# Layer 0's first four token blocks in a written-out order, and the products beside the latents dealt out anew

## The chip, the cores and the metric

The kernel runs on one core of a Trainium2 chip. The metric is the device time of one execution in microseconds (us); lower is better. The core's engines work beside each other: TensorE (PE, with its weight loads shown as PEld), VectorE (DVE), ScalarE (ACT), GpSimd (POOL) and SyncE (SP), which issues most of the DMAs. Each works through its own instructions in the order in which they were written and waits on semaphores for the others.

## The reference, cut to what matters

Two layers over 4 sequences of 256 tokens with 512 features (1024 tokens, eight blocks of 128). What the change touches is at the start of layer 0 and, with one list of numbers, at the second half of its tokens:

```
x = L0_attn_x                         # (4, 256, 512)
xn = _layernorm(x, axis=-1)
x = x + _L0_attn_ref(xn, ...) + _L0_ffn_ref(xn, W_gate, W_up, W_down)
xn = _layernorm(x, axis=-1)
x = x + _L1_attn_ref(xn, ...) + _L1_ffn_ref(xn, ...)

# _L0_attn_ref
C_q = x @ Wq_d + bq_d                 # 12 latent features
C_kv = x @ Wkv_d + bkv_d              # 4 latent features
q = (C_q @ W_qk + b_qk).reshape(b, s, 32, 4)
scores = einsum('bqhd,bkd->bhqk', q, C_kv) / sqrt(4)
out = einsum('bhqk,bkhd->bqhd', softmax(scores), V)
# _L0_ffn_ref
h = silu(x @ W_gate.T) * (x @ W_up.T) # 1792 hidden features
out = h @ W_down.T
```

Layer 1 is a selective scan (a state-space block) and a mixture of low-rank experts. The change does not touch it.

## The kernel before

**Tiling.** Layer 0 handles the tokens in two halves (`th` 0 and 1) of four blocks of 128. A half is two sequences (`b` 0, 1 and 2, 3). The order of every instruction is written out by hand: Python calls and generators give it, and `go(gen, n)` takes `n` steps of a generator.

**First four blocks** (lines 534 to 549). Each block of `x` is normalized: `ln_stats` (DVE: statistics L207, L208), `ln_root` (ACT: square root, L212), `ln_scale` (DVE: reciprocal L218, `xn` L221). `ln_turn` has PE turn the block in four transposes (L243) into a PSUM tile `pt`, and ACT copies it out twice: `xhi` (L245, rounded for the fast product type) and `xnT` (L246, whole). `ln_rest` (L252, DVE) writes `xlo`, the difference of `pt` and `xhi`. Products of the feed-forward read `xhi` and `xlo`; the latents read `xnT`. The PSUM pool `psmm` has three buffers of tag "mm", which `pt`, the latents' products and the feed-forward's share; `pssc` has two of tag "sc" for score products.

**The latents** (`latents(b)`, L289) are a generator of nine steps for one sequence: `pl` (L294, four products that need two blocks of `xnT`) with its copies on ACT (`kT` L297, `ks` L298, `cq` L300); the split of the key on DVE (`ks`, L302); `pkm` (L307) and its copy `km` (L308); `pq` (L313) with `q`, `qhi` on ACT (L317, L320); `qlo` on DVE (L322) and `pz` (L327); and four times `pqg` (L336) with its copy `qg` (L338). Before, the first step of the first latents stands inside the loop over blocks, behind the turn of block 2 and ahead of the turn of block 3.

**The feed-forward** `ff` is a generator too. In the first half it is `gate_up(0)` (L431): one step is one pair of products `pg` or `pu` (L445, `xhi` and `xlo` with one chunk of weights); four steps fill one PSUM tile, then ACT and DVE make `g` (L452, L453, L455), ACT `hhi` (L456) and POOL `hlo` (L457). The weights `wgu` come by POOL's DMAs into four buffers, three tiles ahead. In the second half, while the latents run, it is `down(0, i)`: one step is a pair `po` (L470), and the first step of a block is the product with `m_att` (L465).

**Maxima** (`maxima`, L559): for eight `k`, two score products `sc` (L353, eight matmuls in all) and their maxima on DVE (L355), a number of steps of `ff` from the list `pieces`, at three `k` a `put_max` (L365, L372), and one step of the second sequence's latents. Then `attention` follows. The totals of `ff` steps up to the attention are 41 in the first half (9 beside the latents, 32 in the maxima) and 35 in the second (9 and 26).

Of the kernel before, what the change touches and what calls it, by code (L numbers as in the profile page):

```python
# [8 lines left out]
F32 = mybir.dt.float32  # L9
# [8 lines left out]
P = 128  # L18
# [3 lines left out]
HC = D // P  # L22
# [19 lines left out]
def block_kernel(  # L42
# [24 lines left out]
    nc = tc.nc  # L67
    mm = nc.tensor.matmul
# [16 lines left out]
    ident = cst[:, C_ID : C_ID + P]  # L85
# [8 lines left out]
    psmm = ctx.enter_context(tc.tile_pool(name="psmm", bufs=3, space=PSUM))  # L94
    ps0 = ExitStack()
    pssc = ps0.enter_context(tc.tile_pool(name="pssc", bufs=2, space=PSUM))
# [79 lines left out]
    def fold_load():  # L176
        live["wvt"] = ffn.tile([P, 4, P], F32, tag="g", name="wvt", bufs=2)
        nc.sync.dma_start(live["wvt"], wvt_d)
        live["wo"] = ap1.tile([P, 4, D], F32, tag="pe", name="wo", bufs=2)
        nc.sync.dma_start(live["wo"], wo_d)  # L180
        nc.sync.dma_start(bo, bo_d)
# [12 lines left out]
    tok = {}  # L194
# [9 lines left out]
    def ln_stats(th, i):  # L204
        mv = tok[th][2]
        st = ap1.tile([P, 6], F32, tag="ln_st", name="st", bufs=2)
        nc.vector.bn_stats(st, x[:, 4 * th + i, :])  # L207
        nc.vector.bn_aggr(mv[:, i, :], st)  # L208

    def ln_root(th, i, n):  # L210
        mv, rs = tok[th][2:]
        nc.scalar.activation(rs[:, i : i + n], mv[:, i : i + n, 1], AF.Sqrt, bias=eps[:, 0:1])  # L212

    def ln_scale(th, i, n):
        mv, rs = tok[th][2:]
        if th == 0 or i == 0:
            m = n if th == 0 else 4
            nc.vector.reciprocal(rs[:, i : i + m], rs[:, i : i + m])  # L218
        for k in range(i, i + n):
            xn = ap1.tile([P, D], F32, tag="ln_xn", name="xn", bufs=2)  # L220
            nc.vector.tensor_scalar(  # L221
                xn, x[:, 4 * th + k, :], mv[:, k, 0:1], rs[:, k : k + 1], ALU.subtract, ALU.mult
            )
            tok[th, k] = xn
# [14 lines left out]
    def ln_turn(th, i):  # L239
        xnT, (hi, lo) = tok[th][:2]  # L240
        pt = psmm.tile([P, HC, P], F32, tag="mm", name="pt")
        for hc in range(HC):
            nc.tensor.transpose(pt[:, hc, :], tok[th, i][:, hc * P : (hc + 1) * P], ident)  # L243
        w = slice(i * P, (i + 1) * P)
        nc.scalar.copy(hi[:, :, w], pt)  # L245
        nc.scalar.copy(xnT[:, :, w], pt)  # L246
        tok[th, i] = pt

    def ln_rest(th, i):
        hi, lo = tok[th][1]  # L250
        w = slice(i * P, (i + 1) * P)
        nc.vector.tensor_tensor(lo[:, :, w], tok[th, i], hi[:, :, w].bitcast(F32), ALU.subtract)  # L252
# [93 lines left out]
    def scores_max(b, k, hp):  # L346

        gq, qb = k // 2, k % 2
        sc = pssc.tile([P, 2, 512], F32, tag="sc", name="sc")
        for hf in range(2):  # L350
            for i in range(2):
                w = rows(2 * hp + i)
                mm(sc[:, i, hf * S : (hf + 1) * S], lhsT=qs[b][w, gq, hf, qb * P : (qb + 1) * P],  # L353
                   rhs=kms[b][w], start=True, stop=True)
        nc.vector.tensor_reduce(  # L355
            mpl2[b % 2][:, qb, 2 * hp : 2 * hp + 2, 16 + 2 * gq : 18 + 2 * gq],
            sc.rearrange("p i (f k) -> p i f k", f=2), AX.X, ALU.max,
        )

    def put_max(b, gq):  # L360


        pm = psmm.tile([P, S], F32, tag="mm", name="pmT")
        for qb in range(2):
            nc.tensor.transpose(  # L365
                pm[:, qb * P : (qb + 1) * P], mpl2[b % 2][:, qb].rearrange("p h r -> p (h r)"),
                ident,
            )
        for hf in range(2):
            g = 2 * gq + hf  # L370
            q = qs[b][:, gq, hf, :]
            nc.vector.scalar_tensor_tensor(  # L372
                q, pm, mask[:, g : g + 1], q.bitcast(F32), ALU.mult, ALU.add
            )
# [56 lines left out]
    def gate_up(th):  # L431


        hi, lo = hids[th]
        xs = tok[th][1]
        for m in range(MC):
            for k in range(2):
                i = th * NW + 2 * m + k
                load_w(i + 3)
                if th == 0 and k == 0 and m % 2 == 1:  # L440
                    nc.gpsimd.dma_start(wd[:, m - 1 : m + 1, :], wd_d[:, m - 1 : m + 1, :])
                ps = psmm.tile([P, 512], F32, tag="mm", name="pg" if k == 0 else "pu")
                for hc in range(HC):
                    for j in range(2):
                        mm(ps, lhsT=wgus[i][:, hc, :], rhs=xs[j][:, hc, :],  # L445
                           start=(hc == 0 and j == 0), stop=(hc == HC - 1 and j == 1))
                    if hc < HC - 1:
                        yield

                if k == 0:  # L450
                    g = ffn.tile([P, 512], F32, tag="g", name="g", bufs=2)
                    nc.scalar.activation(g, ps, AF.Tanh, scale=0.5)  # L452
                    nc.vector.scalar_tensor_tensor(g, g, 1.0, ps, ALU.add, ALU.mult)  # L453
                else:
                    nc.vector.scalar_tensor_tensor(g, g, 0.5, ps, ALU.mult, ALU.mult)  # L455
                    nc.scalar.copy(hi[:, m, :], g)  # L456
                    nc.gpsimd.tensor_tensor(lo[:, m, :], g, hi[:, m, :].bitcast(F32), ALU.subtract)  # L457
                yield
# [26 lines left out]
    def go(gen, n=1000):  # L485
        for _ in range(n):
            if next(gen, 1) == 1:
                break
# [7 lines left out]
    def attention(b, ff, after, step, side=()):  # L496


        side = dict(side)
        for k in range(8):  # L500
            attend(b, k, 0)
            if after:
                scores_max(b + 1, k, 1 - k // 2 % 2)
            elif k:
                attend(b, k, 1)
            if after or k == 0:
                go(ff, step - step // 2)
            if k == 0:
                put_max(b, 3)
                go(ff, 3)  # L510
            elif after and k in (3, 5, 7):
                put_max(b + 1, k // 2 - 1)
            if after or k == 0:
                attend(b, k, 1)
            if after:
                scores_max(b + 1, k, k // 2 % 2)
            if k:
                weigh(b, k - 1)
            elif b % 2:
                weigh(b - 1, 7)  # L520
            go(ff, step // 2 if after or k == 0 else step)
            for f, *args in side.get(k, ()):
                f(*args)
# [12 lines left out]
        ln_stats(0, i)  # L536
        ln_root(0, i, 1)
    first, second = latents(0), latents(1)
    for i in range(4):
        ln_scale(0, i, 1)  # L540
        ln_turn(0, i)
        if i == 2:
            go(first, 1)
        if i < 2:
            ln_stats(0, i + 2)
            ln_root(0, i + 2, 1)
        if i:
            ln_rest(0, i - 1)
    ln_rest(0, 3)
    nc.scalar.preload_act_table_set("exp_and_others")  # L550
    fold_load()
    for tb in range(4, NTB):
# [3 lines left out]
    ff = gate_up(0)  # L556
    masks()

    def maxima(b, pieces, second, side=()):  # L559

        side = dict(side)
        for k in range(8):
            for hp in range(2):
                scores_max(b, k, hp)
            for f, *args in side.get(k, ()):
                f(*args)
            go(ff, pieces[k])
            if k in (3, 5, 7):
                put_max(b, k // 2 - 1)
            go(second, 1)  # L570
        go(second)

    for _ in range(9):
        go(first, 1)
        go(ff, 1)
    maxima(0, (5, 5, 1, 6, 1, 5, 5, 4), second, {2: [(fold_att, 0)], 4: [(fold_att, 1)]})
    attention(0, ff, True, 5)
    norm = normalize(0)
    attention(1, ff, False, 3, {
# [9 lines left out]
    ff = (0 for i in range(4) for _ in down(0, i))  # L589
# [5 lines left out]
    for i in range(4):  # L595
        ln_turn(1, i)
        if i == 1:
            ln_scale_act(1, 2, 2)
        go(ff, 3)
        ln_rest(1, i)  # L600
    first, second = latents(2), latents(3)
    for i in range(9):
        go(first, 1)
        go(ff, 1)
        if i == 5:
            pre_stats(0)
    maxima(2, (4, 3, 3, 5, 3, 3, 3, 2), second, {
        2: [(pre_stats, 1)], 3: [(pre_scale,)], 5: [(pre_turn, 0)], 7: [(pre_turn, 1)],
    })
    go(ff)  # L610
# [1 line left out]
    ff = gate_up(1)  # L612
# [742 lines left out]
    ff = (0 for i in range(4) for _ in down(1, i))  # L1355
# [407 lines left out]
    for u in range(total + 2):  # L1763
# [6 lines left out]
        elif u > total:  # L1770
            b, c = B - 1, DC - 1
# [111 lines left out]
```

## Time and profile before

| | us |
|---|---|
| median of 3 runs | 820.84 |
| lowest, highest | 815.27, 824.40 |
| the profiled execution, its own time | 817.16 |
| its span | 814.9 |

The profile is of one execution. Its span counts from the first to the last instruction; its own time is 2.3 us longer. Times in the text are counted from the span's start. The stages by the windows of the trace: the first blocks and latents to 32.0 us, maxima of sequence 0 to 65.1, attention and feed-forward of the first half to 151.5, latents of the second half to 165.9, their maxima to 194.6, the rest of layer 0 and the entry of layer 1 to about 345, and layer 1's scan to the end.

How to read it: a line of the timeline gives start, duration, engine, line of the code, operation, tiles and shapes, and in brackets the idle time before it with what ended it. `L294` is line 294. A record of PE stands for one pass, so the four products of `pl` show as eight. The granted clock is the rate that TensorE's throttle let through, 1.00 being full speed.

### The profile page before, as it was taken

Reading aid. Unit: us, or ns where it says so; the run is one execution under the profiler, and the core shown is the slowest. Engines: PE = TensorE matmul, PEld = TensorE weight load, DVE = VectorE, ACT = ScalarE, POOL = GpSimd, SP = SyncE. Lnnn points to the kernel's source line nnn. Section 1 sums busy time; section 2 is a strip of 40 time slices with the busy share of each in tenths; the row PEclk is TensorE's granted clock in tenths of the full one; section 3 lists DMA queues with packets and bytes.
Section 4 is the critical chain, followed back from the end, with each engine's and each line's share of the span. In section 5 each row is a group of like instructions: output and inputs, shape, how many; then the busy total and the mean of one; then the engine's idle time right before and its main releaser. Section 6 shows DMA issues by size and latency. Waiting matters only on the chain.

```text
span 814.9 us, 11167 instructions
## 1 busy us (share of the span) xinstructions
PE 722.6 (89%) x3778; PEld 424.3 (52%) x3778; DVE 653.3 (80%) x589; ACT 552.2 (68%) x1122; POOL 515.8 (63%) x419
## 2 busy tenths in 40 slices
PE   4999999999999999989788888799888779889876
PEld 2665545566555586656446456454356345334331
DVE  4486756368654525998999999999999999999996
ACT  4335565434556347789998898989978897955642
POOL 4133232001333351758998999989799999889875
PEclk9799999999999999999979799899999889999989
DMA  7233432000322433366677627544547553464610
GB/s 232 65 93 90 130 91 77 1 1 14 78 78 78 120 65 104 103 164 191 186 186 196 177 68 200 142 106 104 180 102 158 119 141 104 117 143 118 127 40 27
DMA packets 72802, 92.02 MB, mean 113 GB/s; under 512 B 12733, under 2 KB 54793, under 8 KB 72618
## 3 DMA queue, kind: packets, MB, share of 16 engines
q1 hardware_dynamic: 61226, 67.98, 31.4%
q0 software_dynamic: 10800, 21.50, 11.1%
q10 hardware_dynamic: 720, 1.84, 0.6%
q8 instruction: 30, 0.49, 0.3%
q14 instruction: 26, 0.21, 0.1%
HBM read 68.67 MB, written 13.43 MB: 101 GB/s over the span
## 4 chain that ended last, share of the span: by engine, by line
PE 40%; DVE 36%; ACT 10%; issue 4%; POOL 4%; DMA 3%; SPq 1%; POOLq 0%; ACTq 0%; DVEq 0%
DVE h L1123 15%; DVE bx L1106 12%; PE pg L445 7%; PE pu L445 5%; DVE x L1123 4%; PE av L398 4%; PE px L793 4%; ACT decay L1091 3%; PE po L470 3%; POOL h L1128 2%; PE scT L387 2%; DVE mpl L355 2%; PE po L1328 2%; PE ysum L1146 1%; DMA dus<-dud 1%
## 5 line engine op out<-in xcount | busy, mean ns | idle before, releaser
L1128 POOL TENSOR_TENSOR h<-h,cr 128x1024 f32<-128x1024 f32 (+1 forms) x105 | 245.6, 2345 | 34.2 <-DVE h L1123 24.1
L1123 DVE TENSOR_TENSOR_SCAN h<-decay,bx 128x1024 f32<-128x1024 f32 (+1 forms) x101 | 224.1, 2222 | 3.6
L1091 ACT ACTIVATE decay<-dts,aneg 128x255 f32<-128x255 f32 x492 | 205.4, 499 | 30.6 <-DVE h L1123 19.1
L1106 DVE TENSOR_TENSOR bx<-brow,dus 128x1024 f32<-128x1024 f32 x128 | 157.6, 1231 | 9.7 <-ACT decay L1091 4.6
L457 POOL TENSOR_TENSOR hlo<-g,hhi 128x512 fp32r<-128x512 f32 x28 | 35.9, 1282 | 114.5 <-ACT hhi L456 114.5
L1146 PE MATMUL ysum<-h,stack 128*32 128x256 f32 x824 | 69.3, 412 | 33.1 <-POOL h L1128 32.7
L355 DVE TENSOR_REDUCE mpl<-sc 128x4 f32<-128x1024 f32 x64 | 76.7, 1218 | 22.6 <-PE sc L353 21.2
L428 POOL DMA_DIRECT2D wgu<-in_wgu x56 | 31.0, 556 | 95.2 <-PE pg L445 94.3
L389 ACT ACTIVATE pe<-scT 128x1024 f32<-128x1024 f32 x64 | 64.0, 1023 | 22.9 <-PE sc L353 14.2
L793 PE MATMUL px<-xn1T,w_in 128*128 128x256 f32 x256 | 63.8, 401 | 8.1 <-ACT xn1T L781 4.0
L1328 PE MATMUL po<-ow,xc 128*128 128x512 f32 x128 | 66.7, 645 | 0.9 <-DVE xc L1776 0.4
L1056 PE MATMUL pz<-xn1T,w_in 128*128 128x256 f32 x256 | 64.6, 399 | 0.6 <-ACT sz L1067 0.6
L1128 POOL TENSOR_TENSOR x<-x,cr 128x1024 f32<-128x1024 f32 x24 | 57.8, 2406 | 6.4 <-DVE x L1123 3.9
L793 PEld LDWEIGHTS px<-xn1T,w_in 128*128 128x128 f32 x256 | 50.2, 200 | 20.8 <-ACT xn1T L781 4.5
L1146 PEld LDWEIGHTS ysum<-h,stack 128*32 128x32 f32 x824 | 18.2, 111 | 78.3 <-POOL h L1128 52.1
L1056 PEld LDWEIGHTS pz<-xn1T,w_in 128*128 128x128 f32 x256 | 49.2, 199 | 18.0 <-issue 8.7
L1123 DVE TENSOR_TENSOR_SCAN x<-decay,bx 128x1024 f32<-128x1024 f32 x24 | 54.9, 2286 | 0.8
L453 DVE SCALAR_TENSOR_TENSOR g<-g,pg 128x512 f32<-128x512 f32 x28 | 19.2, 687 | 43.0 <-ACT g L452 43.0
L445 PE MATMUL pg<-xhi,wgu 128*128 128x512 f32 x112 | 49.6, 443 | 1.2 <-ACT xhi L245 1.2
L470 PE MATMUL po<-wd,hhi 128*128 128x512 f32 x112 | 49.6, 443 | 0.0
L456 ACT CAST hhi<-g 128x512 fp32r<-128x512 f32 x28 | 17.3, 619 | 45.8 <-DVE g L455 45.8
L445 PE MATMUL pu<-xhi,wgu 128*128 128x512 f32 x112 | 47.5, 424 | 0.8 <-DVE g L455 0.8
(244 smaller groups left out, 1399.6 us busy)
## 6 DMA issues: line engine op xcount, KB each, us to landing
dts<-dtd SPq DMA_DIRECT2D x124, 128.0 KB, 3.0
dus<-dud SPq DMA_DIRECT2D x124, 128.0 KB, 3.3
wgu<-in_wgu POOLq DMA_DIRECT2D x56, 256.0 KB, 2.8
w_in<-in_inz SPq DMA_DIRECT2D x16, 512.0 KB, 5.2
w_in<-in_inx SPq DMA_DIRECT2D x14, 512.0 KB, 4.4
dtd<-dt SPq DMA_DIRECT2D x15, 256.0 KB, 2.6
dud<-du SPq DMA_DIRECT2D x15, 256.0 KB, 2.2
wd<-in_wd POOLq DMA_DIRECT2D x7, 512.0 KB, 3.5
```

The costliest lines, as they stand in the source:

```text
L355: nc.vector.tensor_reduce(mpl2[b % 2][:, qb, 2 * hp : 2 * hp + 2, 16 + 2 * gq : 18 + 2 * gq], sc.rearrange("p i (f k) -> p i f k", f=2), A ...
L389: nc.scalar.activation(pes[b, k][:, 2 * t : 2 * t + 2, :], sc, AF.Exp)
L445: mm(ps, lhsT=wgus[i][:, hc, :], rhs=xs[j][:, hc, :], start=(hc == 0 and j == 0), stop=(hc == HC - 1 and j == 1))
L470: mm(po, lhsT=hids[th][j][:, m, i * P : (i + 1) * P], rhs=wd[:, m, :], start=False, stop=(m == MC - 1 and j == 1))
L793: mm(px[:, i, :], lhsT=w[:, i, hc, :], rhs=xns[b][:, hc, :], start=(hc == 0), stop=(hc == HC - 1))
L1056: mm(pz[:, i, :], lhsT=w[:, i, hc, :], rhs=xns[b][:, hc, :], start=(hc == 0), stop=(hc == HC - 1))
L1091: made["da", u] = nc.scalar.activation(da[:, k, 1:], live["dts", b, c][:, k, 1:], AF.Exp, scale=aneg[:, c, k, g : g + 1])
L1106: nc.vector.tensor_tensor(bx, brow[g // 2][:, g % 2, :].unsqueeze(1).to_broadcast([P, NG, S]), live["dus", b, c], ALU.mult)
L1123: nc.vector.tensor_tensor_scan(h[:, n].rearrange("p n t -> p (n t)"), da[:, n].rearrange("p n t -> p (n t)"), bx[:, n].rearrange("p n t -> ...
L1128: made["hc", u] = (nc.vector if k == NG - 1 else nc.gpsimd).tensor_tensor(h[:, n], h[:, n], crows[b][:, g, :].unsqueeze(1).to_broadcast([P ...
L1146: made["sum", u] = mm(ysum[k * NB : (k + 1) * NB, :], lhsT=stack, rhs=hc[:, k, :], start=False, stop=(g == NU - 1))
L1328: mm(live["po", b, i], lhsT=xcs[b][:, c, i * P : (i + 1) * P], rhs=late_w["ow"][:, c, :], start=first, stop=last)
```

## The change

Three new functions split `ln_turn` for the first half: `first_turn` (PE's transposes alone; block 3 takes its PSUM tile from the "sc" buffers), `first_high` (the copy `xhi`) and `first_whole` (the copy `xnT`). The loop over the four blocks is replaced by a written-out order in which all four turns come before the first step of the latents. The steps of `ff` beside the latents are no longer one each: 3, 0, 1, 2, 2, 1, 1, 1, 1 (and 0 for an extra last step in the first half, since the latents' first step has moved there). Beside the latents there are now 12 steps of `ff` in either half, and three fewer in the maxima, one less at `k` 0, 3 and 6.

```
+    def first_turn(i):
+        if i < 3:
+            pt = psmm.tile([P, HC, P], F32, tag="mm", name="pt")
+        else:
+            pt = pssc.tile([P, 2, 512], F32, tag="sc", name="pt")[:, 0, :].rearrange(
+                "p (c k) -> p c k", c=HC
+            )
+        for hc in range(HC):
+            nc.tensor.transpose(pt[:, hc, :], tok[0, i][:, hc * P : (hc + 1) * P], ident)
+        tok[0, i] = pt
+
+    def first_high(i):
+        nc.scalar.copy(tok[0][1][0][:, :, i * P : (i + 1) * P], tok[0, i])
+
+    def first_whole(i):
+        nc.scalar.copy(tok[0][0][:, :, i * P : (i + 1) * P], tok[0, i])
...
-    for i in range(4):
-        ln_scale(0, i, 1)
-        ln_turn(0, i)
-        if i == 2:
-            go(first, 1)
-        if i < 2:
-            ln_stats(0, i + 2)
-            ln_root(0, i + 2, 1)
-        if i:
-            ln_rest(0, i - 1)
+    ln_scale(0, 0, 1)
+    first_turn(0)
+    ln_stats(0, 2)
+    ln_root(0, 2, 1)
+    ln_scale(0, 1, 1)
+    first_high(0)
+    first_turn(1)
+    ln_stats(0, 3)
+    ln_root(0, 3, 1)
+    first_high(1)
+    ln_scale(0, 2, 1)
+    first_turn(2)
+    first_whole(0)
+    ln_scale(0, 3, 1)
+    first_turn(3)
+    ln_rest(0, 0)
+    first_high(2)
+    ln_rest(0, 1)
+    first_whole(1)
+    first_high(3)
+    ln_rest(0, 2)
     ln_rest(0, 3)
+    first_whole(2)
+    first_whole(3)
...
-    for _ in range(9):
+    for n in (3, 0, 1, 2, 2, 1, 1, 1, 1, 0):
         go(first, 1)
-        go(ff, 1)
-    maxima(0, (5, 5, 1, 6, 1, 5, 5, 4), second, {2: [(fold_att, 0)], 4: [(fold_att, 1)]})
+        go(ff, n)
+    maxima(0, (4, 5, 1, 5, 1, 5, 4, 4), second, {2: [(fold_att, 0)], 4: [(fold_att, 1)]})
...
-    for i in range(9):
+    for i, n in enumerate((3, 0, 1, 2, 2, 1, 1, 1, 1)):
         go(first, 1)
-        go(ff, 1)
+        go(ff, n)
         if i == 5:
             pre_stats(0)
-    maxima(2, (4, 3, 3, 5, 3, 3, 3, 2), second, {
+    maxima(2, (3, 3, 3, 4, 3, 3, 2, 2), second, {
```

## The prediction

> **What bounds the kernel now.** I read the page's busy shares first, then its windows cut by stage and, around the changed places, by the steps of the granted clock, then the order of time of these places. Busy times stand behind each stretch as length, PE, PEld, DVE, ACT, POOL, then granted clock, DMA share, GB/s.
>
> ```profile
> PE 722.6 (89%) x3778; PEld 424.3 (52%) x3778; DVE 653.3 (80%) x589; ACT 552.2 (68%) x1122; POOL 515.8 (63%) x419
> ```
> ```profile
> 12.29:15.70 3.41, 3.41 (x10) 1.51 (x9) 0.69 (x1) 0.92 (x2) 0.00 (x0) 1.00 1.34 386
> 15.70:19.11 3.41, 1.35 (x5) 0.49 (x3) 1.37 (x5) 3.12 (x6) 0.00 (x0) 1.00 0.04 10
> 19.11:22.53 3.42, 3.18 (x7) 1.95 (x7) 0.09 (x1) 0.37 (x1) 0.00 (x0) 0.50 0.00 0
> 22.53:25.94 3.41, 3.41 (x10) 1.99 (x9) 0.87 (x2) 1.46 (x3) 0.00 (x0) 0.50 0.00 0
> 25.94:29.36 3.42, 3.42 (x14) 2.80 (x13) 0.69 (x1) 1.38 (x3) 0.54 (x1) 0.50 0.27 77
> 29.36:32.00 2.64, 2.64 (x17) 2.08 (x16) 0.35 (x1) 1.57 (x3) 0.00 (x0) 1.00 0.00 0
> 32.00:65.10 33.10, 31.90 (x179) 20.95 (x178) 27.48 (x34) 11.38 (x21) 11.22 (x15) 1.00 0.34 96
> ...
> 159.06:162.47 3.41, 3.18 (x7) 1.82 (x7) 1.65 (x5) 0.59 (x1) 0.00 (x0) 0.50 0.00 0
> ...
> 165.90:194.64 28.74, 27.56 (x166) 19.05 (x165) 24.41 (x31) 9.26 (x17) 0.00 (x0) 1.00 0.00 1
> 194.64:345.00 150.36, 147.04 (x745) 93.63 (x745) 86.28 (x114) 88.44 (x148) 57.90 (x79) 1.00 0.32 84
> 345.00:814.90 469.90, 395.21 (x2091) 220.85 (x2090) 447.17 (x299) 373.55 (x836) 413.03 (x261) 0.93 0.53 135
> ```
> ```profile
> 11.58 3.64 PE L294 MATMUL pl<-xnT,wlat 128*40 128x256 f32 x8
> ...
> 17.68 0.69 DVE L252 TENSOR_TENSOR xlo<-pt,xhi 128x512 fp32r<-128x512 f32 x1 [4.19 <-ACT xnT L246]
> ...
> 18.79 0.41 DVE L302 TENSOR_TENSOR ks<-kT,ks 8x256 fp32r<-8x256 f32 x1
> ...
> 19.35 0.55 PE L307 MATMUL pkm<-ks,selk 40*128 40x256 f32 x1 [0.42 <-DVE ks L302]
> ...
> 32.00 0.52 PE L353 MATMUL sc<-km,qg 32*128 32x256 f32 x8
> ...
> 34.94 1.92 PE L294 MATMUL pl<-xnT,wlat 128*40 128x256 f32 x8
> ```
>
> To 345 us PE is the longest engine in every stage after the start (147.04 of 150.36 us from 194.64 on); from 345 on DVE is (447.17 of 469.90). The stages hang on each other, so a microsecond won on PE early is a microsecond at the end, if nothing gives it back. Two things are lost before 32 us. PE is busy 1.35 of 3.41 us between 15.70 and 19.11, waiting for the fourth block, its rest (17.68) and, queued behind that rest on DVE, the key split (18.79). Then three stretches of 3.41 us run at clock 0.50 although PE is nearly always busy. The first clock record is at 15.70, so the 1.00 in rows before it is only the lack of one: the first `pl` took 3.64 us, the second 1.92 (34.94), four transposes 1.11 at 6.83 and 0.60 at 142.08. PE started at half speed, was raised after a stretch full of `pl` and dropped after the sparse one.
>
> **The change, part by part.** No arithmetic is added or removed. A pair is what one step of `ff` gives PE: two products, 0.46 us at full clock. ACT's eight block copies (0.59 each, 0.48 apart), DVE's four rests (0.69, 0.60 apart), 16 transposes and all loads remain; SP's and POOL's instructions stand in the same order. The fourth turn takes an `sc` buffer, so it no longer waits for a PSUM buffer of the three.
>
> First four blocks. I carry the rows forward with their gaps. Statistics of block 3 end at 9.04; without the rest of block 0 in between, the scale of block 2 starts at 9.13 (before 9.89), its turn runs 9.73 to 10.84 (before 10.53); scale 3 at 9.78, turn 3 on its heels to 11.6 (before 15.15 to 16.05). ACT: high 0 at 7.98, high 1 at 9.43, whole 0 at 9.91, high 2 at 10.88. The rests are queued behind both scales: rest 0 at 10.54, rest 1 at 11.14. In the built order whole 1 waits for rest 1 (to 11.83), so it runs 11.87 to 12.46, and `pl`, which reads it, starts at 12.50, 0.92 us later than before: that is this part's price. High 3 is done at 12.94, rest 3 at 13.67, whole 3 at 14.3, ACT's table load (1.28) at 15.5, DVE's masks before that, all under `pl`. That takes seven eighths of itself by 15.70 at 0.455 a record and ends at 15.95, if the raise comes there as before (at full clock throughout it would end at 14.4, and the table load would be last: kT 0.5 earlier). Then ACT's kT (0.56 to the next), ks (0.40) and the split (0.41) end at 17.39, and `pkm` starts at 17.53: 1.82 earlier. Six `pg` (0.23 each, 1.38) now lie under that chain; nothing is before them on DVE. The first four weight blocks had landed by 16.1, where DMA falls silent; POOL issues the fifth when pg is emptied (18.6) and the sixth behind the first hlo (25.1), and at 2.6 to 6.4 us to landing both are there before their use after 30. By `pkm` six products are done rather than two: four more, 0.92. Part one: 2.74 us.
>
> From `pkm` to the first score product. Before: 12.65 us (19.35 to 32.00), with 8 pairs of products. After, at full clock, with 9 pairs, prices from the second half's rows (154.93 to 165.90): pkm to pg 0.28, that pair 0.66 with the gap behind it, so pq at 18.47, 1.06; four `pu` to 20.55. Here a new wait: pz needs the buffer that DVE's g empties (tanh 18.59, g to 19.91): it is covered. pz 0.64, four `pu` to 22.2; meanwhile q8, its high and low parts (0.84, 0.62, 0.69) end at 21.85, so the first pqg finds them ready. ACT's hhi (after DVE's second g, 23.12) now stands ahead of the first qg copy, so the third pqg waits to 24.3, the fourth to 25.25; the score product starts at 26.3. That is 8.77 us; the ninth pair is worth 0.46; part two: 12.65 + 0.46 - 8.77 = 4.34. Most of it is clock: the same rows cost 9.85 us between 19.9 and 29.75 and 5.5 at full clock.
>
> Does the clock hold? In stretches of 3.41 us, columns of 128-row products that PE streams come to some 57% of what full clock could stream in 15.70 to 19.11 (eight pg and the end of `pl`), 59% in the next, 76% in the third; of those in the trace, one at about 30% (155.65 to 159.06: four po and a pqg, the rest pq and pz with 12 and 8 rows) was followed by half clock, one at 16% too (15.70), and none above some 40%. [...]
>
> Maxima of batch 0. Three pairs (1.38 us of PE) have left, one each from k 0, 3 and 6: 29 in place of 32. Bounds: all of it comes off (1.38), or none, because DVE's reductions (18.80) were what ran last. PE was busy 31.90 and DVE 27.48; with 30.5 against 27.5 PE is still the longer, so I take all. Part two and one already count the pairs as done, so nothing more is added.
>
> Layer 1's latents. `pl` to the first score product is 14.43 us before (151.47 to 165.90) with 9 pairs; after, three pairs fill 153.32 to 154.8 where PE waited 0.41 for the split; the m_att product (1.88) now lies between pq and pz, so pqg never waits for the low part (0.23 before), and the stretch after 155.65 holds that product and is no longer sparse: the half-clock stretch at 159.06 goes (2.85 us for the m_att rows against 1.88). Worked through, the score product stands at 164.95 with 12 pairs: 0.95 + 1.38 = 2.33. In its maxima, 23 pairs for 26, PE falls from 27.56 to 26.2 beside DVE's 24.41 in 28.74; here they are closer, and I take 1.0 of 1.38 as kept: minus 0.38.
>
> Sum: 2.74 + 4.34 + 2.33 - 0.38 = 9.0 us. Against its own time, 817.16 (span 814.9 and 2.3 around it), that is 808.2; it lies 3.7 below the median of 820.84, which gives 811.8.
>
> **Rivals.**
> *The clock falls again (0.14).* PE's stalls between 17.4 and 18.5 and the thin pq and pz leave one stretch too sparse; half clock then lasts two or three stretches. For it: those gaps exist. Against: 57% beside the 30% that fell. Two to three stretches give back 2.9 to 4.3 us of part two; at 3.5 the gain is 5.5, 815.3.
>
> *DVE bounds both maxima stages (0.12).* The pairs moved are work from under the reductions, and none comes off: gain 9.0 - 1.38 - 1.0 = 6.6, 814. For it: 32.6% of the chain of waits in the second stage lies on L355; against: DVE idles 5.6 and 4.3 us there.
>
> *A busy window is enough (0.04).* If any stream reopened the clock after one stretch, as the rows say it did not here, executions of before would lose one stretch and not three: two thirds of 4.3 us vanish from the gain, 2.9: gain 6.1, 814.7. [...]
>
> *Slower (0.08).* With fewer pairs between them, PE waits on DVE before each score pair, and stretches of the maxima become sparse. Each half-clock stretch costs half of 3.41, 1.7 us; the two stages hold 61.8 / 3.41 = 18. Beyond (9.0 + 8.2) / 1.7 = 10 of them the kernel is over 1% slower; with 12 it is 820.84 - 9 + 20.5 = 832. Against: 3 pairs are 3072 columns of 33 us, a 4% thinner stream, and not one of these 18 is at half clock now.
>
> **How the numbers follow.** The forecast has 0.62, with a spread of 7.5 to 13 us, upward because the sum takes no later half-clock stretch as saved (1.7 us each). One per cent, 8.2 us, is what a measurement of this kernel can tell from no change. Of the forecast 0.56 lies above it and 0.06 below; of the three rivals at 814 to 815.3, 0.04 above and 0.26 below: faster 0.60, same 0.32, slower 0.08. Range: the low end takes 13 us and runs as far below the median as the lowest shown can be in part (3 us): 804; the high end takes the rivals at 814 to 815 and the 3.6 by which the highest run exceeds the median: 819.
>
> **What would show it.** Right: granted clock 1.00 from about 16 us on without a drop; `pkm` near 17.5, first score product near 26.3, the second half's 2.3 us shorter. Wrong: a row of 0.50 between 17 and 27, `pl` later than 13, or a maxima stage as long as before with fewer pairs in it.

## The result and the profile after

The changed kernel took 813.98 us (median of 13 executions, 808.31 to 818.6) beside 817.39 for the kernel before (13, 815.21 to 824.4). The ratio is 0.9936, 95% interval 0.9912 to 0.9959, that is 3.4 to 7.2 us won with 5.2 in the middle (the two medians alone lie 3.4 apart). The interval leaves out 1, so the changed kernel is faster, but by less than the 1% that the prediction took as the least that can be told from no change. The direction and the range held; the gain was put too high, 9.0 us forecast.

The profiled execution of the changed kernel took 808.31 us, the lowest of its 13; its span is 806.5, 8.4 below the 814.9 before. First the page's busy shares after, then its windows (length, PE, PEld, DVE, ACT and POOL busy, granted clock, DMA share, GB/s), then the order of time.

```profile
PE 714.1 (89%) x3778; PEld 418.9 (52%) x3778; DVE 651.8 (81%) x589; ACT 552.4 (69%) x1122; POOL 516.1 (64%) x419
```
```profile
12.17:15.58 3.41, 3.06 (x8) 1.35 (x8) 1.32 (x5) 3.12 (x5) 0.00 (x0) 1.00 1.27 371
15.58:19.00 3.42, 3.41 (x14) 2.06 (x13) 0.42 (x1) 2.22 (x6) 0.22 (x1) 1.00 0.00 0
19.00:22.41 3.41, 3.41 (x17) 2.32 (x16) 1.47 (x3) 1.57 (x4) 0.32 (x1) 1.00 0.28 77
22.41:26.43 4.02, 4.02 (x25) 2.92 (x23) 0.69 (x1) 2.54 (x5) 2.35 (x3) 1.00 0.00 0
26.43:59.08 32.65, 30.48 (x172) 19.77 (x171) 27.16 (x33) 11.09 (x21) 8.90 (x12) 1.00 0.34 98
145.41:158.77 13.36, 13.36 (x60) 8.66 (x60) 3.27 (x7) 5.29 (x11) 0.00 (x0) 1.00 0.00 0
158.77:187.05 28.28, 26.03 (x161) 17.64 (x161) 24.47 (x31) 9.16 (x17) 0.00 (x0) 1.00 0.00 1
303.19:806.50 503.31, 427.14 (x2234) 241.95 (x2234) 470.76 (x324) 398.67 (x896) 430.85 (x281) 0.93 0.52 131
```
```profile
12.52 3.35 PE L311 MATMUL pl<-xnT,wlat 128*40 128x256 f32 x8 [0.59 <-ACT xnT L264]
...
17.47 0.35 PE L324 MATMUL pkm<-ks,selk 40*128 40x256 f32 x1
...
26.43 0.52 PE L370 MATMUL sc<-km,qg 32*128 32x256 f32 x8
```

The first score product stands at 26.43 (32.00 before), the sparse stretch is full (3.41 of 3.42 us from 15.58 on) and no stretch of 0.50 follows in layer 0. But both stages of maxima, the rows 26.43 and 158.77, are hardly shorter (33.10 and 28.74 before), though three pairs have left each. Layer 1 starts (first `px`) at 282.33 for 289.87: 7.54 us won in layer 0. The remaining 0.86 of the 8.4 is the scan of layer 1 (503.31 for 504.17), where both kernels run the same instructions.

### The profile page after: what moved, and what is told of

Its sections match the earlier page's. It is cut to its first block, busy times and chain, and to the rows that moved or that the text cites. A ratio compares the mean times of both kernels' runs of the same rounds, so it can differ in the third digit from the quotient of the medians.

```text
span 806.5 us, 11165 instructions
## 1 busy us (share of the span) xinstructions
PE 714.1 (89%) x3778; PEld 418.9 (52%) x3778; DVE 651.8 (81%) x589; ACT 552.4 (69%) x1122; POOL 516.1 (64%) x419
## 4 chain that ended last, share of the span: by engine, by line
PE 41%; DVE 26%; ACT 12%; POOL 9%; issue 5%; DMA 4%; SPq 1%; POOLq 0%; ACTq 0%; DVEq 0%
DVE h L1153 10%; DVE bx L1136 8%; PE pg L462 6%; PE pu L462 6%; POOL h L1158 5%; ACT decay L1121 5%; PE po L487 4%; PE av L415 4%; PE px L823 3%; DVE mpl L372 3%; DVE x L1153 3%; PE scT L404 2%; PE ysum L1176 2%; PE pp L914 2%; PE po L482 1%
## 5 line engine op out<-in xcount | busy, mean ns | idle before, releaser
L1176 PE MATMUL ysum<-h,stack 128*32 128x256 f32 x824 | 67.8, 406 | 34.3 <-POOL h L1158 34.2
```

Source lines behind the costliest of these rows:

```text
L1176: made["sum", u] = mm(ysum[k * NB : (k + 1) * NB, :], lhsT=stack, rhs=hc[:, k, :], start=False, stop=(g == NU - 1))
```

## The experiments

Places of fourteen traces (the two kernels and twelve runs), in us from the span's start; "raised" is where the first record of granted clock 1.00 starts, until which PE ran at half speed (the first four transposes took 1.11 us ahead of it in the changed kernel and 0.60 behind it in e7), "half" is the time at granted clock 0.50 from there to the first `scT`, "second half" runs from its `pl` to the first `scT` and stands with a * where a half-clock stretch of 3.4 us lies in it. The ratio is to the kernel before, timed beside each, with its 95% interval.

| kernel | raised | `pkm` | first `sc` | half | first `scT` | second half | `px` | scan | ratio |
|---|---|---|---|---|---|---|---|---|---|
| before | 15.70 | 19.35 | 32.00 | 10.2 | 65.10 | 43.17* | 289.87 | 504.2 | |
| before again (e12) | 15.24 | 19.46 | 31.88 | 10.2 | 65.06 | 42.98* | 289.62 | 504.0 | |
| changed | 15.46 | 17.47 | 26.43 | 0 | 59.08 | 41.64 | 282.33 | 503.3 | 0.9936 (0.9912–0.9959) |
| changed again (e4) | 18.35 | 19.04 | 28.02 | 0 | 60.73 | 41.66 | 283.97 | 505.4 | 0.9928 (0.9899–0.9956) |
| e1 order | 15.85 | 17.71 | 28.96 | 6.8 | 62.03 | 41.64 | 285.25 | 508.6 | 0.9972 (0.9944–1.0) |
| e2 first dealing | 15.63 | 20.28 | 34.51 | 17.1 | 68.72 | 41.65 | 291.99 | 505.4 | 0.9981 (0.9953–1.001) |
| e3 second dealing | 15.87 | 19.69 | 32.28 | 10.2 | 65.44 | 41.64 | 288.65 | 505.1 | 1.0005 (0.9982–1.0029) |
| e5 unread products | 13.90 | 18.74 | 30.72 | 6.8 | 63.81 | 42.92* | 288.35 | 503.4 | 0.9998 (0.9976–1.0019) |
| e6 late block | 15.21 | 21.04 | 34.33 | 13.6 | 68.55 | 41.62 | 291.61 | 508.4 | 1.0039 (1.0019–1.0059) |
| e7 early clock | 7.64 | 17.83 | 26.77 | 3.4 | 61.02 | 41.63 | 284.28 | 508.2 | 0.9946 (0.9924–0.9968) |
| e8 early clock, fewer pairs | 5.71 | 16.94 | 24.50 | 0 | 58.00 | 41.62 | 281.28 | 507.2 | 0.9899 (0.9868–0.993) |
| e9 fewer pairs | 18.17 | 18.70 | 26.27 | 0 | 59.81 | 41.63 | 283.02 | 507.7 | 0.9894 (0.9864–0.9925) |
| e10 fewer in both halves | 18.61 | 18.92 | 26.52 | 0 | 60.02 | 40.74 | 282.38 | 502.9 | 0.9898 (0.9871–0.9925) |
| e11 all of it | 8.04 | 16.00 | 23.59 | 0 | 57.07 | 40.72 | 279.38 | 512.7 | 0.9912 (0.9883–0.9941) |

The first `sc` compares only kernels with as many pairs ahead of it: 12 in the changed kernel, e2, e6 and e7, 9 in before, e1, e3 and e5, 8 in e8 to e11. `scT` compares all.

**e1, the written order alone.** The changed kernel with every step of `ff` dealt as before:

```
-    for n in (3, 0, 1, 2, 2, 1, 1, 1, 1, 0):
+    for n in (0, 1, 1, 1, 1, 1, 1, 1, 1, 1):
-    maxima(0, (4, 5, 1, 5, 1, 5, 4, 4), ...
+    maxima(0, (5, 5, 1, 6, 1, 5, 5, 4), ...
```
and the second half likewise.

> The written-out order alone, the products dealt as before in both halves. The changed kernel stood 5.6 us ahead at the first score product with three pairs more behind it (26.43 against 32.00), and 7.5 at layer 1's first products. Theory A, the clock: most of that is half clock avoided, and it takes both parts, since with one pair a step the stretches of 3.41 us from 15.5 to 22 hold only 30 to 40% of full-row columns: pkm near 17.5, then a drop to 0.50 for two or three stretches, first score product at 29.5 to 31, and some 2 us shorter than before in all. Theory B, the order's own waits: the blocks' copies out of the key chain are the gain, the clock stays at 1.00 without the new dealing, and the score product comes at 27 or earlier, 5 us shorter in all.

Windows of this run, columns as above:

```profile
15.85:19.26 3.41, 2.48 (x9) 1.32 (x9) 0.41 (x1) 1.71 (x4) 0.00 (x0) 1.00 0.00 0
19.26:22.67 3.41, 3.41 (x10) 1.89 (x9) 0.85 (x2) 1.46 (x3) 0.00 (x0) 0.50 0.00 0
22.67:26.10 3.43, 3.43 (x13) 2.81 (x14) 0.70 (x2) 1.19 (x2) 0.53 (x1) 0.50 0.30 76
26.10:28.96 2.86, 2.86 (x17) 2.24 (x17) 0.35 (x1) 1.76 (x3) 0.00 (x0) 1.00 0.01 1
...
161.24:189.98 28.74, 27.56 (x167) 19.05 (x166) 24.41 (x31) 9.26 (x17) 0.00 (x0) 1.00 0.00 1
```

`pkm` comes 1.64 earlier than before, so the order works alone. PE is busy 2.48 of 3.41 us in the stretch around `pkm`, more than before's 1.35, yet two stretches of 0.50 follow: with two `pg` under the key's chain in place of six the clock falls. The score product at 28.96 is half a us before theory A's range. The last row is the second half's maxima with the old 26 pairs: 28.74 us, to the hundredth as before.

**e2, the first dealing alone**, in the old order: `go(ff, 3)` ahead of the loop and the changed numbers in it and in the first maxima.

> The first half's new dealing alone, on the old order of the blocks (three pairs behind pl and the fourth turn, then 0, 1, 2, 2, 1, 1, 1, 1, 0; maxima with 29 pairs); second half as before. Theory A: PE still idles until the last rest at 18.4, so the clock drops at about 19 as before, but denser stretches bring it back one or two stretches earlier: score product at 29 to 31 with three pairs more, 2 to 3 us shorter in all. Theory B: the pairs only change places, score product at 33 (1.4 later for three pairs more), no difference or up to 0.9 us longer for what the maxima do not give back.

```profile
19.16:22.58 3.42, 3.42 (x8) 1.70 (x8) 0.00 (x1) 0.91 (x2) 0.28 (x1) 0.50 0.00 0
22.58:25.99 3.41, 3.41 (x9) 1.82 (x7) 1.11 (x2) 1.52 (x4) 0.25 (x1) 0.50 0.31 77
25.99:29.40 3.41, 3.41 (x12) 2.80 (x12) 0.64 (x3) 0.00 (x0) 0.00 (x0) 0.50 0.00 0
29.40:32.82 3.42, 3.42 (x14) 3.03 (x14) 0.49 (x1) 1.69 (x3) 2.13 (x3) 0.52 0.00 0
```

A miss for both theories: 34.51, where A had 29 to 31 and B 33. (The stretches of these rows, as of those of the changed kernel and of e6, stand 0.12 us behind the clock's own steps, hence 0.52 in the last one.) Behind the late fourth block the six `pg` do not fill the gap: the first waits for that block's copy until 17.18 and the second for its rest until 18.38, the last two run at half clock ahead of `pkm`, and the half clock lasts four stretches in a row. By `scT` the dealing alone cost 3.62 us in this trace, the order alone won 3.07, both together won 6.02 (4.37 in e4). The parts do not add; they work through the clock.

**e3, the second half's dealing alone**, in the kernel before.

> The second half's new dealing alone, everything else as before. By the changed kernel's trace this half gained 1.53 us (1.07 to its first score product with three pairs more, 0.46 of the pairs' 1.38 back in the maxima). Theory A: the stretch of half clock at 159 goes with it, and the whole is 1.0 to 1.6 us shorter wherever the blank stretch fell before. Rival: the gain belongs to where the 3.41 us stretches happened to lie, and the time is the same within 0.5 us.

No difference in the time (1.0005), though an interval of some 2 us either way could not show the 1.0 to 1.6 expected. The second half takes 41.64 us with the new dealing here and 41.64 with the old one in e1. Only where a half-clock stretch falls into it, as in before, e12 and e5, is the old dealing 1.3 to 1.5 longer; it did so in three of five traces with the old dealing (not in e1 and e2), and in none of the seven that have the changed kernel's second dealing. That it is the new dealing and not chance is borne out by the share of full-row work (counted in the last section): the sparsest stretch of the second half's latents has 32 to 34% with the old dealing, at the edge where the clock dropped, and 46 to 63% with the new.

**e4, the changed kernel once more,** beside e1 to e3 on one chip.

> The changed kernel once more, for a second trace. Its profiled execution took 808.31, the lowest of 13, and the median was 813.98. Theory A: layer 0 is alike in all executions (score product at 26.4, layer 1's first products near 282, within 0.5 us), and the 3 to 6 us between executions lie in the scan of layer 1, which came out at 517 us from px to pp on in one case and longer in others, with other stretches of half clock. Rival: the clock drops early in most executions and the profiled one was lucky: a 0.50 between 15 and 30 us and a score product at 28 or later.

The clock was raised at 18.35 here and not at 15.46; `pl` began 0.6 later and took 3.63 us, and `pkm` came at 19.04. From there to the score product it took 8.98, as in the first trace (8.96). So part one of the gain is not fixed (2.80 us in the first trace, 1.23 here), and part two was the same in both traces. The late raise is no exception: of the six traces with the written-out order and no zeros it came by 15.9 in three (changed, e1, e6) and after 18.1 in three (e4, e9, e10), while in the five with the old order, whose `pl` starts 0.6 to 1.6 us earlier, it always came by 15.9.

**e5, unread products in the kernel before:** `fill(11)` behind DVE's masks and `fill(3)` at the third step of the latents, each product streaming weights that lie there anyway.

> The kernel before, its order and dealing unchanged, with products added on PE that nobody reads: eleven of 512 columns between the fourth turn and the first pg, where PE idled until 19.3, and three between pq and pz. They are extra work (14 x 0.23 us) and take no wait away. Theory A, the clock: PE is no longer sparse from 15.7 to 19.1 and after, the clock stays at 1.00 or drops for one stretch instead of three; pkm as before or up to 0.5 later, but the first score product at 28 to 30 in place of 32.0 to 32.3, and the whole 2 to 4 us shorter in layer 0. Theory B, waits of the order: added work can only cost; score product at 32 to 33.

In between, so it tells little: half clock for two stretches in place of three, the score product 1.3 us earlier in spite of 3.2 us of extra products, and no difference in the whole.

**e6, the late fourth block put back** into the changed kernel, by six copies on ACT that nothing reads:

```
+    late = ap1.tile([P, D], F32, tag="ln_xn", name="late", bufs=2)
+    for _ in range(6):
+        nc.scalar.copy(late, x[:, 3, :])
     (ahead of fold_load())
```

> The changed kernel with six copies of a block added on ACT ahead of the key's chain (six times 0.48 us after the table load, nobody reads them), so that kT comes 2.6 us later and PE has nothing to do from about 17.3 to 20. Theory A: beyond the 2.6 us the stretch from 15.5 or the next one becomes sparse, the clock drops to 0.50, and the score product moves from 26.4 to 30.5 or later (4 us or more). Theory B: the delay alone, score product at 29.0 (2.6 later), clock at 1.00.

```profile
18.75:22.16 3.41, 1.12 (x4) 0.66 (x5) 0.42 (x1) 2.46 (x7) 0.00 (x0) 0.98 0.00 0
22.16:25.57 3.41, 3.41 (x8) 2.11 (x8) 0.69 (x1) 1.98 (x4) 0.54 (x1) 0.50 0.28 77
25.57:28.99 3.42, 3.42 (x11) 2.42 (x10) 0.87 (x2) 0.00 (x0) 0.00 (x0) 0.50 0.00 0
28.99:32.40 3.41, 3.41 (x14) 3.07 (x13) 0.69 (x1) 1.69 (x3) 1.69 (x2) 0.52 0.00 0
32.40:34.33 1.93, 1.93 (x13) 1.47 (x12) 0.00 (x0) 0.95 (x2) 0.66 (x2) 1.00 0.66 197
```

The clearest of the tests: 34.33, as theory A has it (30.5 or later; theory B 29.0). The copies delay `pkm` by 3.57 us and leave one stretch with 1.12 us of PE; the instructions behind `pkm` are the same as in the changed kernel and take 13.29 in place of 8.96, with three stretches at 0.50. The clock is worth 4.33 us here, and the kernel is slower than before (1.0039, 1.0019 to 1.0059).

**e7, the clock raised early:** ten passes of zeros (`fill(5)`) ahead of the first turn, two passes behind turns 0 and 1 each, six behind turn 3, and ACT's table load behind the first step of the latents.

> The changed kernel with products of a zeroed tile that nobody reads on PE from 2.1 us on, before and between the turns and behind the fourth, and ACT's table load moved behind the copies of pl, so that it does not stand before kT. If the clock is raised by PE's being busy whatever it multiplies, it is at 1.00 by about 9 us, pl takes 1.9 us and not 3.4, and pkm and all behind it come 1.3 us earlier (score product near 25.1), in every execution, since it no longer matters where pl falls among the stretches of 3.41 us. If zeros do not count, pl takes 3.4 or more, and the result is that of the changed kernel within 0.3 us.

```profile
2.13 6.74 PE L561 MATMUL warm<-zk 128*128 128x448 f32 x10 [2.13 <-POOL zk L142]
...
8.71 0.60 PE L257 MATMUL pt<-cst,xn 128*128 128x128 f32 x4
...
14.31 1.92 PE L311 MATMUL pl<-xnT,wlat 128*40 128x256 f32 x8
```

The clock was up at 7.64 us, and `pl` took 1.92 us instead of 3.35. But the ten passes, most of them at half clock (their weight loads start 0.75 us apart up to 7.52, and 0.38 apart in the passes behind turn 3), took 6.74 us, the first turn waited for them until 8.71, and `pl` began 1.8 later: the score product at 26.77 misses the 25.1 expected and is no gain on the first trace of the changed kernel.

**e8 and e9, fewer pairs beside the latents.** Since the pairs moved out of the maxima had given back a third of their time (below), four were put back, the first three staying under the key's chain: e8 on top of e7, e9 on the changed kernel.

```
-    for n in (3, 0, 1, 2, 2, 1, 1, 1, 1, 0):
+    for n in (3, 0, 1, 2, 2, 0, 0, 0, 0, 0):
-    maxima(0, (4, 5, 1, 5, 1, 5, 4, 4), ...
+    maxima(0, (5, 5, 2, 6, 1, 5, 5, 4), ...
```

> As e7_warm, with 8 pairs beside the first half's latents in place of 12 (none with the four pqg) and 33 in its maxima (5, 5, 2, 6, 1, 5, 5, 4). The maxima took 33.1 us with 32 pairs and 32.65 to 32.71 with 29, so 0.15 us a pair where PE needs 0.46: DVE's reductions bound them. Then four pairs moved there cost 0.6 and save 1.84 beside the latents: the attention starts 1.2 us before e7_warm's. Rival: with 33 pairs PE is the bound (30.5 + 1.9 of 32.7) and nothing or up to 0.4 us is won; or the thin stretch with pqg alone drops the clock.

> The changed kernel, its order kept, with 8 pairs beside the first half's latents and 33 in its maxima, nothing else (no products on the zeroed tile, the table load where the change has it). From e8_lean's trace four pairs moved back cost the maxima 0.85 us (33.50 against 32.65) and leave 1.84 free ahead of them: the attention starts 1.0 us earlier after pl than the changed kernel's 46.56. The clock: with pqg alone after 22 us the stretches hold some 45% of full-row columns; theory A says it stays at 1.00 above 40%. Rival: it drops there and the first score product comes later than 26.4.

From `pkm` to `scT` e9 takes 41.11 us, the changed kernel 41.61 and 41.69, e8 41.06 and e7 43.19 (a half-clock stretch): 0.5 won where 1.0 was expected, again half. Counted from `pl`, as the expectation has it, e9 takes 47.14 us and the changed kernel 46.56 and, raised as late as e9, 47.59 (e4). e8's `scT` is 3.0 us before e7's and not 1.2, but 1.6 of that is e7's half-clock stretch and 0.9 an earlier `pl`. Both kernels are faster than the one before, 0.9894 and 0.9899; their intervals touch those of the changed kernel, so whether they beat that one isn't settled.

**e10 and e11, the same in the second half; then e10 with six passes of zeros ahead of the first turn, two behind the fourth, and the table load placed as in e7.** The second half's numbers are (3, 0, 1, 2, 2, 0, 0, 0, 0) and (4, 4, 3, 5, 3, 3, 3, 2).

> e9_deal8 with the second half dealt alike: 8 pairs beside its latents, 27 in its maxima (4, 4, 3, 5, 3, 3, 3, 2). With 9 pairs and with 12 that half took 41.64 us from pl to the attention, whichever way. If what bounds it is the hand-over between PE and DVE's reductions, four pairs moved into the maxima cost them little and win up to 1 us; by the two values that are known, nothing (41.6).

> e10_both8 with three products of the zeroed tile ahead of the first turn (five delayed that turn from 7.0 to 8.7 us, because each took 1.35 us at half clock) and one behind the fourth turn, and the table load behind the copies of pl. Raised by 6 to 9 us, the clock lets pl start at 12.5 and take 1.92; first score product near 23.5, 3 us before the changed kernel's, and the whole some 2.5 to 3 us shorter than the changed kernel. Rival: between the turns PE is too sparse, the clock falls again before pl, and pl takes 3.4 us.

The second half falls from 41.64 to 40.74, 0.9 of the 1 us that the theory of the hand-over gave at most. e11 has its first score product at 23.59, as expected, and the shortest layer 0 of all, `px` at 279.38, 2.95 before the changed kernel, and yet the longest scan, 512.7: its lead is gone at the end.

**e12, the kernel before again.**

> The kernel before once more, for a second trace of it. If the half clock of its first half is a matter of its order and not of chance: 0.50 from about 19 to 29 us and the first score product at 32 to 32.5, as in the first trace and in e3_deal2, whose first half is the same. If the second half's dealing is worth nothing by itself: 41.64 us from its pl to the attention here too, unless a stretch of half clock falls there (43.17 with one). Layer 1 from its first pp product to the end: 503 to 505 us, or 507 and more if the half clock at some 145 us into it lasts 13.7 us and not 10.2.

`pkm`, score product and `scT` repeat the first trace to within 0.13 us, and the half clock lasts 10.2 us again; a half-clock stretch falls into the second half too (42.98). So what stands in the table against it is not one odd execution.

## Why the prediction was right or wrong

**The first four blocks: right in size, not fixed in place.** `pkm` at 17.53 forecast, 17.47 measured, with `pl` at 12.52 for 12.50 and four products more: 2.80 for 2.74. That the raise came "as before" was luck: e4, e9 and e10 have it some 3 us later. In e4, with the raise 2.9 us later and the first `pl` 0.6 later, the same code gives 1.23 (0.31 at `pkm` and the 0.92). The forecast named the raise as a condition and priced the later start of `pl` at 0.92 us; it gave no price to the raise being missed, which befell three of the six traces with the written-out order, its later `pl` and no zeros, and none of the five with the old order.

**From `pkm` to the score product: right.** 8.77 forecast, 8.96 and 8.98 measured; 4.34 and 4.15 of gain. That most of it is clock is shown by e6, which takes exactly these instructions back to 13.29.

**The clock holds: right, and by the forecast's own count.** It counted full-row columns and put 57, 59 and 76% in three stretches as enough; counted the same way (see the last section), the trace has some 57, 50 and 82% from 15.46 on. e1 has two `pg` where the changed kernel has six, 28% in the stretch at 15.85, and falls; e6 has all six but an almost empty stretch, 12%, and falls. Neither the order nor the dealing is enough. On the rival that a busy window is enough, e6's rows 22.16 and 25.57 are decisive: PE is busy 3.41 of 3.41 us by its records and the clock stays at 0.50 for a stretch after each. What the change avoids is a drop of the clock behind the raise; e6 prices it at 4.33 of 817 us, 0.5%, and that was most of the change.

**The pairs that leave the maxima: the mis-sized term.** The step that failed reads "PE is still the longer, so I take all". It took 1.38 us off the first stage and kept 1.0 of 1.38 in the second. Measured: 33.10 to 32.65, 0.45, and 28.74 to 28.28, 0.46. The missing 0.93 and 0.54 are 1.47 us, and 9.0 less 1.47 is the 7.54 found at `px`. The busy totals had said that PE (30.48) stays above DVE (27.16), and that is so; but 30.48 is not 32.65. PE now idles 2.17 us in the first stage where it idled 1.20, and 2.25 in the second for 1.18. What PE waited for on DVE's reductions in the second stage, by the view of PE's waits (total us, times, longest), before and in the changed kernel:

```profile
PE pmT L365 <- DVE mpl L355: 0.7, 2, 0.4
PE sc L353 <- DVE mpl L355: 0.4, 1, 0.4
```
```profile
PE pmT L382 <- DVE mpl L372: 1.3, 2, 1.0
PE sc L370 <- DVE mpl L372: 0.8, 2, 0.4
```

They grew by 1.0 us, which is about what did not come off (1.38 less 0.46). In the first stage the same view, before and in the changed kernel, has for `pmT` (the transposes of the maxima):

```profile
PE pmT L365 <- DVE mpl L355: 0.2, 1, 0.2
```
```profile
PE pmT L382 <- DVE mpl L372: 1.2, 2, 0.9
```

Again 1.0 more. It is 1.2 in every trace with 29 pairs (changed kernel, e2, e4, e6, e7) and 0.2 or 0.3 with 32 or 33 (before, e1, e8, e9); in the second stage it is 1.3 with 23 pairs and 0.7 with 26 (before, e1) or 27 (e10). e1, with the new order and the old pairs, has the stages at 33.07 and 28.74 us, which puts the difference down to the pairs. PE, relieved of them, came earlier to the places where it needs the reductions' results, and stood there; on the chain of waits of the second stage DVE's reductions went from 32.6 to 49.2%. (On that of the first stage they went from 21.6 to 18.7%, so there only the waits carry the argument.) The totals hid this because they add up a whole stage, and the wait sits at a few places in it. A pair of 0.46 us gave back 0.15 when it left, and the four that e9 puts back lengthen the stage by 0.22 each (33.54). The rival that DVE bounds these stages outright is wrong in the other direction: a third did come off.

**The second half's latents: right size, other meaning.** The forecast gave 2.33 and, with the maxima, 1.95; measured 2.45 and 1.53. e3 and e1 show that all of it is the half-clock stretch that fell there before, which the forecast had going at a price of 0.97 us (2.85 less 1.88): with the clock up, the new dealing is worth 0.00 us (41.64 and 41.64). The three pairs cost the latents 0.46 (12.90 in e1, 13.36 after) and give 0.46 back in the maxima.

**Slower: its mechanism exists, at a small price.** Neither trace of the changed kernel lost its clock in the maxima. But e2, e6 and e7, which have its 29 pairs in the first stage, each show one half-clock stretch there between 52 and 64 us, and the stage takes 34.2 us in place of 32.65: 1.6 a stretch, as the rival priced it (1.7). With 32 or 33 pairs none of the nine traces shows one. It needed more than ten such stretches to turn the result, and there was one at most. But three of the five traces with 29 pairs have it, a price that no term of the sum held.

**The total.** 808.2 was forecast for the profiled execution, which took 808.31, but not by the forecast's sum: 1.47 us less in layer 0 was nearly made up by 0.86 in the scan and 0.45 outside the span (1.81 us for 2.26). That the number fits is luck. So is part of the range's fit: 804 to 819 was laid out from 820.84, a median of three executions, and the median of thirteen is 817.39. The gain of 5.2 us is about that of the rivals (5.5 to 6.6) and not the 9.0 of the sum, and it falls to the outcome "same", which had a chance of 0.32. The median's gain of some 5 us lies nearer to e4, whose `px` is 5.9 earlier than before's.

## What to carry to other kernels

Where two engines hand results to each other, as PE and DVE do in the maxima, moving work out of the stage can give back less than the busy totals say (here 0.45 of 1.38 us) even though one engine stays the longer: look for the places where it needs the other's result, and at the idle time that stands there already. A change in the order of work and a change in what fills its gaps should be costed together wherever the clock can fall between them; alone, by the traces, one of these two won 3.07 us by the first `scT`, half of the 6.02 of both, and the other lost 3.62. And before a difference of 5 us is read from two profiles, lay the stages that run the same instructions in both side by side: the spread found there is the measure of what one profile can show.

## What the runs showed of the hardware

**The scan of layer 1 has two lengths for the same instructions.** In 14 traces it took 502.9 to 505.4 us in eight and 507.2 to 512.7 in six (e1, e6, e7, e8, e9, e11). One small instruction tells them apart: the first `sel<-dl,b` of the router, 128x32 on DVE, took some 0.30 us in each of the eight and 4.24 to 4.60 in each of the six. In the six, a half-clock run some 145 us into the scan had also lasted 13.7 us in place of 10.2, ending a few us before. The timeline around that instruction (start, length, engine) in the changed kernel, and in e1, DVE and POOL alone:

```profile
465.17 1.27 POOL L1042 TENSOR_TENSOR e<-u,e 128x512 f32<-128x512 f32 x1
466.18 0.31 DVE L1241 TENSOR_TENSOR sel<-dl,b 128x32 f32<-128x32 f32 x1
466.43 2.35 POOL L1158 TENSOR_TENSOR h<-h,cr 128x1024 f32<-128x1024 f32 x1
```
```profile
471.06 1.57 POOL L1042 TENSOR_TENSOR e<-u,e 128x512 f32<-128x512 f32 x1
471.67 4.54 DVE L1241 TENSOR_TENSOR sel<-dl,b 128x32 f32<-128x32 f32 x1
472.30 2.64 POOL L1158 TENSOR_TENSOR h<-h,cr 128x1024 f32<-128x1024 f32 x1
474.60 1.55 POOL L1044 TENSOR_TENSOR e<-e,lw 128x512 f32<-128x512 f32 x1
```

In the changed kernel `sel` ends at 466.49, as POOL's `e` does (466.44). In e1 it lasts until 476.21, through three instructions of POOL that follow each other without a gap, the last ending at 476.15. In e9 it is the same: 471.92 beside 471.86. That POOL's work is what holds `sel`, and that the longer half clock leads to it, was not shown: no run moved POOL's work away from `sel`. Which of the two lengths the executions without a profile had is not known, nor where the 4 us come from by which e11's scan exceeds the other five long ones.

**Busy records of PE did not bring the clock back.** At 0.50 for 10.2 us (before, e6) and 13.7 us (e2), PE was busy all along, save 0.24 us in before. In each of these runs the stretch after which the clock rose is the one with the most products in it (x14 in the rows, after x7 to x12), and products of zeros raised it in e7 (at 7.64 us, with nothing but them on PE from 2.13 on).

**The share of full-row work tells the stretches apart.** This is an estimate, from the columns and starts of PE's records in the first 300 us of all fourteen traces: the columns of 128-row products in each stretch of 3.41 us, as a share of what full clock could stream, taken as twice the 512 in 0.43 us of the half clock (products that take twice as long per column count double, such as `pl`, of which before starts 256 columns every 0.43 us at half clock, where e6 starts 512 of `pu`; and the four `av` that run side by side, starting within 0.02 us of each other at 73.91 in before, count as one). At full clock the 13 stretches that were followed by 0.50 have 12 to 33%, and the 1141 that were not have 33% or more. At half clock, where 50% is the most there can be, the 51 stretches that did not bring the clock back have at most 38% and the 27 that did at least 41%. It also fits the late raise: the stretch that ends near 15 us has 36 to 38% in e4, e9 and e10 and 41 to 47% in the changed kernel's first trace, e1 and e6. No run set this share by itself, so what lowers and raises the clock stays open.
